# Where the blank rows and the zeros live: a tile moved from the prep's memory to the scatter stage's memory, with its stores

## The chip, the cores and the metric

The kernel runs on one core of one Trainium2 chip. The metric is device time in microseconds (us) of one execution; the median of 10 runs before the change is 7055.33 us (lowest 7051.05, highest 7059.59). Engines are written as the profile writes them: PE (matmul), DVE (vector), ACT (scalar), POOL (GpSimd) and SP (which here only issues transfers). KB in the profile's lists are 1024 bytes; MB and GB/s are decimal.

## The reference, cut to what matters

Four graph layers are computed one after another on 12,500 nodes with 128 features and 200,000 edges; each ends in a layer norm. Only the first layer matters here. It is a weighted sum over edges, grouped by the edge's source node, of rows looked up at the edge's destination node:

```python
def weighted_midpoint_spmm(x_hyp, c, rows, cols, vals):      # rows = src, cols = dst (sorted), vals = edge_weight
    gamma = 2.0 / jnp.clip(1.0 - c * jnp.sum(x_hyp * x_hyp, axis=-1, keepdims=True), EPS)
    gx = gamma * x_hyp
    num = jax.ops.segment_sum(vals[:, None] * gx[cols], rows, num_segments=N_NODES)
    den = jax.ops.segment_sum(vals * (gamma[:, 0] - 1.0)[cols], rows, num_segments=N_NODES)[:, None]
    ...
    return mobius_scalar_mul(0.5, num / den, c)

x = _layernorm(x + _L0_gnn_ref(x, src, dst, edge_weight), axis=-1)
...
```

Layer 2 has a mixture of experts, whose rows are later gathered through a DRAM buffer that must begin as zeros.

## The kernel before

Nodes are held in 98 tiles (`NT`) of 128; edges in 391 blocks (`NB`) of 512. The first layer runs in three stages, one after another.

**Prep** (function `spread_edges`, L489 to L634, and its generator `points`, L452 to L487). The index arrays are loaded, turned to columns by PE transposes (`columns`, L540) and cut into node tile and place within it. A small DRAM round trip (`first_d` stored at L580, read back as `first_r` and `tile_r` at L581 and L583) gives every partition the first node of each block. `rows_d` (L629) puts the rows of indices in DRAM. Then `points` computes the squares of all node rows (`sq`, L469, with sums on DVE at L470), some column arithmetic, and the lookup table `table0`: 14 groups of 7 node tiles, each cut into three bf16 parts (`parts`, L278 to L288: casts on ACT at L283, L285 and L287, differences on DVE at L284 and L286) and stored from SP at L450. The tiles of this loop have two buffers, so that group g+2 starts when the store of group g has landed.

**Scatter** (L636 to L770). For each block of 512 edges: `fetch` (L654) loads the block's indices (`rb`, 256 KB, L656) and 128 rows of the table (`win`, 96.8 KB, L661), both from SP, four buffers each; `places` compares and ranks on DVE; PE picks the rows with one-hot matmuls (L695, L701); ACT casts them into message rows (L734); POOL writes them with four indirect transfers (L751), 128 rows of 792 bytes each, into the DRAM array `msg`. There, each of the 98 source tiles has room for 18 x 128 rows, of which the edges fill only some.

**Collect** (`collect_edges`, L850). All 98 pieces of `msg` are loaded back (`ce_r`, L860) and summed. The first of these loads follows the last scatter.

Rows of `msg` that no edge fills must hold a neutral row. That is the work of the tile `blank` (L516 to L519: four 128-row blocks of zeros, with -1 and 127 in the last columns) and of `clear` (L521 to L524), which stores it with one SP transfer of 396 KB. The last tile's three stores come first (L633 and L634; they cover its blocks 8 to 17), and every other tile's last four blocks are cleared by one call each in `fetch` (L662 to L667). Scatters of the first half of the blocks (`i < MID`) are declared free of a dependence on the clears made in `fetch`, so the scheduler may put these anywhere among them; the first scatter does depend on the last tile's three stores. In the same way the tile `zero` (L639 and L640) is stored 56 times, 448 KB each, into the experts' buffer `buf` (L668 to L670), from SP.

In the scatter loop the order of DVE, PE and ACT is written out by hand (`manual_schedule`, L710). SP and POOL are not in that list: a scheduler orders their transfers, and hoists a store as soon as its source tile is ready in its estimate. A tile's memory matters for that: a tile of the pool `sc` (`pc`) has memory of its own from the start of the prep; a tile of a pool opened after the prep's pools `px` and `rf` are closed takes over memory that these have used, and must wait until it is free.

Of the kernel before, what the change touches and what calls it, by code (L numbers as in the profile page):

```python
# [10 lines left out]
F32 = mybir.dt.float32  # L11
BF16 = mybir.dt.bfloat16
# [6 lines left out]
PSUM = bass.MemoryType.PSUM  # L19
DRAM = bass.MemoryType.DRAM  # L20

P = 128
N = 12500
D = 128
# [11 lines left out]
W0 = D + 2  # L36
# [11 lines left out]
RB = 18  # L48
SURE = 14
SURE_LAST = 8  # L50
RS = RB * P
# [6 lines left out]
W3 = 3 * W0 + 6  # L58
# [80 lines left out]
def gnn_kernel(ctx: ExitStack, tc: tile.TileContext, a, out: bass.AP):  # L139
    nc = tc.nc  # L140
    V, S, G, T, Y = nc.vector, nc.scalar, nc.gpsimd, nc.tensor, nc.sync
# [53 lines left out]
    msg = dram.tile([NMSG, W3], BF16, name="msg")  # L195
# [293 lines left out]
    def spread_edges(bad):  # L489
# [5 lines left out]
        with tc.tile_pool(name="sc", bufs=1) as pc, tc.tile_pool(name="scp", bufs=1, space=PSUM) as pps:  # L495
# [16 lines left out]
            V.memset(rows, 0.0)  # L512
            V.memset(rows[:, :, :, D + 1:D + 2], 1.0)


            blank = pc.tile([P, RB - SURE, W3], BF16, name="blank")  # L516
            V.memset(blank, 0.0)
            V.memset(blank[:, :, 3 * W0:3 * W0 + 1], -1.0)
            V.memset(blank[:, :, 3 * W0 + 1:3 * W0 + 3], 127.0)  # L519

            def clear(t, b0, b1):  # L521
                r0 = t * RS
                return Y.dma_start(msg[r0 + b0 * P:r0 + b1 * P, :].rearrange("(b p) f -> p b f", p=P),
                                   blank[:, 0:b1 - b0, :])  # L524

            if True:
                px_ = ExitStack()
                pt = points(px_.enter_context(tc.tile_pool(name="px", bufs=1)), px_)
# [1 line left out]
                with tc.tile_pool(name="rf", bufs=1) as pa, tc.tile_pool(name="rfp", bufs=2, space=PSUM) as tp_:  # L530
# [25 lines left out]
                    f = pa.tile([P, NBK, EB], F32, name="f_r")  # L556
# [73 lines left out]
                    columns(w_c, w_r)  # L630
                next(pt, None)
                px_.close()
                for b in range(SURE_LAST, RB, RB - SURE):  # L633
                    clear(NT - 1, b, min(b + RB - SURE, RB))  # L634

            with tc.tile_pool(name="sb", bufs=4) as lp, tc.tile_pool(name="sw", bufs=3) as wk, \  # L636
                    tc.tile_pool(name="sg", bufs=2, space=PSUM) as gp:
                step = 7 * D
                zero = pc.tile([P, step], F32, name="zero")  # L639
                V.memset(zero, 0.0)  # L640
                bz = buf[0:DUMP, :].rearrange("(p r) f -> p (r f)", p=P)
                empty = list(range(NT - 1))
                fill = list(range(0, DUMP // P * D, step))
# [10 lines left out]
                def fetch(i):  # L654
                    rb[i] = lp.tile([P, 2 * EB], BF16, name="rb")
                    Y.dma_start(rb[i], rows_d[i].partition_broadcast(P))  # L656
                    _, at = nc.values_load_multi_w_load_instructions(
                        first_r[0:1, i:i + 1], engines=[ET.SP], min_val=0, max_val=NP - 1,
                        skip_runtime_bounds_check_because="clamped to the last node on the chip")
                    win[i] = lp.tile([P, 3, D + 1], BF16, name="win")  # L660
                    Y.dma_start(win[i].rearrange("p k f -> p (k f)"), table0[ds(at[0], P), :])  # L661
                    if 4 <= i < MID - 20 and empty:  # L662

                        for _ in range(-(-NT // (MID - 24))):
                            cl = clear(empty.pop(0), SURE, RB)
                            tc.declare_no_dep(cl.ins, group="spread", reason="rows that no edge has yet")
                            tc.add_to_no_dep_group("blank", cl.ins)  # L667
                    if i % 6 == 5 and fill:  # L668
                        r = fill.pop(0)
                        Y.dma_start(bz[:, r:r + step], zero)  # L670
# [331 lines left out]
    with tc.tile_pool(name="cei", bufs=1) as pi:  # L1002
        ih_i = pi.tile([P, WM], I16, name="ih_i")
        G.iota(ih_i, pattern=[[1, WM]], base=-(WM // 2), channel_multiplier=0)
        V.tensor_copy(iota_h, ih_i)
    spread_edges(bad)
    places_ = ctx.enter_context(ExitStack())
    plp = places_.enter_context(tc.tile_pool(name="places", bufs=1, side="right"))
# [602 lines left out]
```

## Time and profile before

| what | value |
|---|---|
| median of 10 runs | 7055.33 us |
| the profiled execution's own time | 7049.75 us |
| its span, first to last instruction | 7048.0 us |
| prep: first table group's arithmetic (L448) starts | 109.23 us |
| scatter stage: first window load issued, first and last scatter start | 203.65, 212.37 and 2195.1 us |
| collect: first load of `ce_r` | 2197.9 us |
| stores of `blank` (L523): number, first and last issue | 100, 31.9 and 402.5 us |
| stores of `zero` (L670): number, first and last issue | 56, 68.7 and 732.9 us |
| memset of `blank` (L517), of `zero` (L640) on DVE | 718 ns, 805 ns |

How to read it: the span is a little shorter than the time, and it is that of one execution. "Busy" counts an engine's instructions, and the DMA share is the mean busy share of 16 DMA engines; it can exceed 1 in a window. Transfers that SP issues are listed as SPq; an issue that has to wait for room shows as a longer issue, or as a wait of SP for an earlier transfer. A releaser behind `<-` names what ended an idle time.

### The profile page before, as it was taken

Reading aid. Unit: us, or ns where it says so; the run is one execution under the profiler, and the core shown is the slowest. Engines: PE = TensorE matmul, PEld = TensorE weight load, DVE = VectorE, ACT = ScalarE, POOL = GpSimd, SP = SyncE. Lnnn points to the kernel's source line nnn. Section 1 sums busy time; section 2 is a strip of 40 time slices with the busy share of each in tenths; the row PEclk is TensorE's granted clock in tenths of the full one; section 3 lists DMA queues with packets and bytes.
Section 4 is the critical chain, followed back from the end, with each engine's and each line's share of the span. In section 5 each row is a group of like instructions: output and inputs, shape, how many; then the busy total and the mean of one; then the engine's idle time right before and its main releaser. Section 6 shows DMA issues by size and latency. Waiting matters only on the chain. (4 is left out here: it accounts for less than half of the span.)

```text
span 7048.0 us, 106823 instructions
## 1 busy us (share of the span) xinstructions
PE 5168.6 (73%) x33009; PEld 3148.9 (45%) x33009; DVE 4277.1 (61%) x11730; ACT 2016.6 (29%) x4176; POOL 3881.9 (55%) x3917
## 2 busy tenths in 40 slices
PE   0566666666664666699998548998809999699995
PEld 0454444444442333355554336664305544355544
DVE  6787777777775778766665574556991223411115
ACT  3343333333331223333332113444440001100003
POOL 0677777777773000577777570004707776477760
PEclk5555555555556888899999559999959999799998
DMA  9996555555557999355554115554458889698872
GB/s 233 245 244 201 164 152 153 153 152 152 153 153 222 326 324 311 122 166 166 166 165 151 46 56 156 166 165 139 141 156 275 292 287 297 206 291 288 282 229 63
DMA packets 1046138, 1375.96 MB, mean 195 GB/s; under 512 B 106733, under 2 KB 848745, under 8 KB 1045567
## 3 DMA queue, kind: packets, MB, share of 16 engines
q1 hardware_dynamic: 803208, 960.67, 46.3%
q0 software_dynamic: 181312, 376.38, 17.6%
q10 hardware_dynamic: 61046, 31.77, 1.6%
q8 instruction: 301, 4.93, 0.3%
q14 instruction: 271, 2.21, 0.1%
HBM read 911.40 MB, written 457.00 MB: 194 GB/s over the span
## 5 line engine op out<-in xcount | busy, mean ns | idle before, releaser
L1134 POOL DMA_INDIRECT fg<-table,e_row x1952 | 1956.5, 1002 | 1513.7 <-SPq L1023 670.5
L1125 PE MATMUL dense<-fc_a,fc_x 128*128 128x512 bf16 x7644 | 1910.4, 381 | 205.8 <-DMA fc_x<-table 205.5
L751 POOL DMA_INDIRECT msg<-rows,to x1564 | 1505.1, 962 | 672.3 <-issue 360.2
L1125 PEld LDWEIGHTS <-fc_x 128*128 128x128 bf16 x7644 | 678.4, 98 | 797.6 <-issue 195.9
L1227 DVE TENSOR_TENSOR AT<-AT,fps 128x512 f32 x122 | 84.0, 689 | 1489.9 <-PE fps L1151 1489.6
L1089 PE MATMUL fb_ps<-fd,fs 128*128 128x512 bf16 (+4 forms) x4108 | 894.0, 343 | 65.9 <-DVE fd L1075 52.3
L734 ACT CAST rows<-g_ps 128x516 bf16<-128x516 f32 x1173 | 699.6, 596 | 708.4 <-PE g_ps L701 329.1
L701 PE MATMUL g_ps<-rows,minus 128*128 128x258 bf16 x1564 | 463.9, 400 | 584.5 <-ACT rows L734 550.3
L695 PE MATMUL g_ps<-win,hot 128*128 128x129 bf16 x4692 | 650.7, 311 | 265.4 <-DMA win<-table 178.7
L1075 DVE TENSOR_SCALAR fd<-iota_h,hd 128x128 bf16<-128x128 f16 (+6 forms) x1563 | 788.7, 509 | 0.0
L1151 PEld LDWEIGHTS <-fg 128*128 128x128 bf16 x5856 | 464.6, 98 | 520.7 <-DMA fg<-table,e_row 91.0
L695 PEld LDWEIGHTS <-hot 128*128 128x128 bf16 x4692 | 533.2, 143 | 347.0 <-issue 212.6
L1151 PE MATMUL fps<-fh,fg 128*128 128x96 bf16 x5856 | 581.7, 208 | 88.0 <-DMA fg<-table,e_row 65.9
L1476 POOL DMA_INDIRECT yk<-ybuf,come x196 | 218.2, 1113 | 653.5 <-DMA counts<-bc_a 594.1
L868 PE MATMUL ce_sum<-ce_r,ce_s 128*128 128x390 bf16 x1764 | 375.9, 379 | 273.7 <-DVE ce_s L865 269.0
L1089 PEld LDWEIGHTS <-fs 128*128 128x128 bf16 x4108 | 377.8, 98 | 374.9 <-issue 110.8
L1091 ACT CAST fc_a<-fb_ps 128x512 bf16<-128x512 f32 x588 | 344.7, 586 | 633.1 <-PE fb_ps L1089 615.6
L701 PEld LDWEIGHTS <-minus 128*128 128x128 bf16 x1564 | 199.6, 128 | 708.4 <-issue 708.2
L679 DVE TENSOR_TENSOR_SCAN run_ps<-one_ps,run_ps,bin 99x512 f32<-99x512 f32 x390 | 505.5, 1296 | 13.8
L1073 DVE TENSOR_SCALAR fs<-iota_b,hs 128x128 bf16<-128x128 bf16 x1563 | 413.3, 267 | 37.8 <-PE fb_ps L1089 34.2
L868 PEld LDWEIGHTS <-ce_s 128*128 128x128 bf16 x1764 | 188.6, 111 | 461.1 <-DVE ce_s L865 261.2
L1091 ACT CAST bc_a<-fb_ps 128x512 bf16<-128x512 f32 x392 | 227.9, 585 | 451.7 <-PE fb_ps L1089 360.3
(382 smaller groups left out, 6268.8 us busy)
## 6 DMA issues: line engine op xcount, KB each, us to landing
ce_r<-msg SPq DMA_DIRECT2D x98, 1782.0 KB
fc_a<-counts SPq DMA_DIRECT2D x196, 768.0 KB
fc_a<-counts SPq DMA_DIRECT2D x196, 512.0 KB
rb<-rows_d SPq DMA_DIRECT2D x391, 256.0 KB
counts<-fc_a SPq DMA_DIRECT2D x98, 768.0 KB
counts<-bc_a SPq DMA_DIRECT2D x98, 512.0 KB
fc_x<-table SPq DMA_DIRECT2D x490, 96.0 KB
msg<-blank SPq DMA_DIRECT2D x99, 396.0 KB
```

What stands on the lines that cost most here:

```text
L679: V.tensor_tensor_scan(c, one_ps, b, st["end"], OP.mult, OP.add)
L695: T.matmul(gps[i][:, q, 0:D + 1], hot[i][:, q * P:(q + 1) * P], win[i][:, k, :], start=(q == 2 * half and k == 0), stop=False)
L701: T.matmul(gps[i][:, 2 * h:2 * h + 2, 0:D + 1], minus, r[:, 2 * h:2 * h + 2, k * W0:k * W0 + D + 1], start=False, stop=True, skip_group_ch ...
L734: S.copy(r[:, :, k * W0:k * W0 + D + 1], gt)
L751: sc = G.indirect_dma_start(out=msg[:, :], out_offset=bass.IndirectOffsetOnAxis(ap=to[:, q:q + 1], axis=0), in_=r[:, q, :], in_offset=None)
L868: T.matmul(ps, sel[:, j, :], r[:, j, 0:3 * W0], start=(j == 0), stop=(j == RB - 1))
L1075: V.tensor_scalar(col[:, 0:hi - lo], iota_h[:, 0:hi - lo], hd[self.i][:, s, q:q + 1], None, op0=OP.is_equal)
L1089: T.matmul(ps[:, lo - c0:hi - c0], self.sel[s, j], self.col[s, j][:, lo - w[j][0]:hi - w[j][0]], start=(j == first), stop=(j == js[-1]))
L1091: S.copy(out[:, c0:c1], ps)
L1125: T.matmul(dense[n], xr[s][:, k, :], cnt[s][:, n * BANK:(n + 1) * BANK], start=(s == 0 and k == 0), stop=(s == NT - 1 and k == 2))
L1134: G.indirect_dma_start(out=g[q][:, i].rearrange("p k f -> p (k f)"), out_offset=None, in_=table[:, :], in_offset=bass.IndirectOffsetOnAxis ...
L1151: T.matmul(ps[:, ds(at[0], LW)], g[i // 4][:, i % 4, k, :], hot[i // 4][:, i % 4, :], start=False, stop=(i == WC - 1 and k == 2))
```

## The change

`blank` and its memsets, `clear` and the last tile's three clears go from the prep's part of the function to the scatter stage's, into a new pool `late` that is opened after the prep's pools are closed; `zero` moves from `pc` into the same pool. Nothing else is edited: the calls in `fetch` stay.

```diff
-            blank = pc.tile([P, RB - SURE, W3], BF16, name="blank")
-            V.memset(blank, 0.0)
-            V.memset(blank[:, :, 3 * W0:3 * W0 + 1], -1.0)
-            V.memset(blank[:, :, 3 * W0 + 1:3 * W0 + 3], 127.0)
-
-            def clear(t, b0, b1):
...
                 next(pt, None)
                 px_.close()
+
+            with tc.tile_pool(name="late", bufs=1) as lt, tc.tile_pool(name="sb", bufs=4) as lp, tc.tile_pool(name="sw", bufs=3) as wk, \
+                    tc.tile_pool(name="sg", bufs=2, space=PSUM) as gp:
+                step = 7 * D
+                zero = lt.tile([P, step], F32, name="zero")
+                V.memset(zero, 0.0)
+
+                blank = lt.tile([P, RB - SURE, W3], BF16, name="blank")
+                V.memset(blank, 0.0)
+                V.memset(blank[:, :, 3 * W0:3 * W0 + 1], -1.0)
+                V.memset(blank[:, :, 3 * W0 + 1:3 * W0 + 3], 127.0)
+
+                def clear(t, b0, b1):
+                    r0 = t * RS
+                    return Y.dma_start(msg[r0 + b0 * P:r0 + b1 * P, :].rearrange("(b p) f -> p b f", p=P),
+                                       blank[:, 0:b1 - b0, :])
+
                 for b in range(SURE_LAST, RB, RB - SURE):
                     clear(NT - 1, b, min(b + RB - SURE, RB))
-
-            with tc.tile_pool(name="sb", bufs=4) as lp, tc.tile_pool(name="sw", bufs=3) as wk, \
-                    tc.tile_pool(name="sg", bufs=2, space=PSUM) as gp:
-                step = 7 * D
-                zero = pc.tile([P, step], F32, name="zero")
-                V.memset(zero, 0.0)
```

In the built program, the order in which SP issues its transfers changes as follows (counts of transfers issued ahead of a given window load; the first four window loads stand next to each other):

| ahead of window load | blank stores before / after | zero stores before / after |
|---|---|---|
| 1 | 53 / 4 | 9 / 0 |
| 5 | 54 / 5 | 9 / 0 |
| 17 | 68 / 23 | 11 / 4 |
| 41 | 97 / 61 | 16 / 10 |
| 65 | 100 / 99 | 29 / 16 |
| 81 | 100 / 100 | 38 / 36 |
| 117 | 100 / 100 | 56 / 56 |

On DVE, the four memsets move from the prep's first part to a place behind the last group's scaling of the table (L448 and L449) and around the first block's comparison `hot` (L674). POOL's order is the same in both. PE and ACT change places only within the prep, and no engine's order changes behind the scatter stage.

More of the change, by code (lines that the diff above doesn't have):

```diff
@@ L513, in spread_edges @@
             V.memset(rows[:, :, :, D + 1:D + 2], 1.0)
-            blank = pc.tile([P, RB - SURE, W3], BF16, name="blank")
-            V.memset(blank, 0.0)
-            V.memset(blank[:, :, 3 * W0:3 * W0 + 1], -1.0)
-            V.memset(blank[:, :, 3 * W0 + 1:3 * W0 + 3], 127.0)
-            def clear(t, b0, b1):
-                r0 = t * RS
-                return Y.dma_start(msg[r0 + b0 * P:r0 + b1 * P, :].rearrange("(b p) f -> p b f", p=P),
-                                   blank[:, 0:b1 - b0, :])
             if True:
```

## Prediction

> **What bounds the kernel now.** I read the slices first, then the rows of the scatter (L751), then tables by stage, then SP's waits, then the timeline of the handover from prep to scatter. The chain of waits is of no use here: followed back from the end it covers only 44% of the span, and its shares hold no prep and no scatter line.
>
> The last two rows of the slices, each 7048.0 / 40 = 176.2 us long, and the scatter's row among the costliest groups:
>
> ```profile
> DMA  9996555555557999355554115554458889698872
> GB/s 233 245 244 201 164 152 153 153 152 152 153 153 222 326 324 311 122 166 166 166 165 151 46 56 156 166 165 139 141 156 275 292 287 297 206 291 288 282 229 63
> L751 POOL DMA_INDIRECT msg<-rows,to x1564 | 1505.1, 962 | 672.3 <-issue 360.2
> ```
>
> The DMA engines are full in the first three slices and 55% busy from the fifth to the twelfth, where POOL paces the scatter. Four indirect transfers make a block; the stretches below count 632 of them in 800 us, so a block takes 4 x 800/632 = 5.06 us (0.96 us of work and 0.30 us of issue, four times). The collect stage starts 2.8 us after the last scatter (2197.9 against 2195.1), so a microsecond lost before the last scatter is a microsecond of span, unless something hides it.
>
> Now the stretches: columns are the stretch, its length, busy us with counts for PE, PEld, DVE, ACT and POOL, then PE clock, DMA share and GB/s.
>
> ```profile
> 800.00:1600.00 800.00, 497.67 (x3792) 385.91 (x3792) 637.29 (x1583) 316.40 (x633) 607.49 (x632) 0.50 0.57 153
> 100.00:200.00 100.00, 0.00 (x0) 0.00 (x0) 59.74 (x90) 44.45 (x48) 0.00 (x0) 0.50 1.01 229
> 207.85:402.07 194.22, 116.49 (x920) 91.19 (x917) 154.58 (x383) 71.98 (x152) 142.41 (x148) 0.50 1.07 254
> 410.00:430.00 20.00, 12.71 (x102) 10.23 (x103) 16.79 (x43) 7.58 (x16) 15.37 (x16) 0.50 1.00 306
> ```
>
> From 207.85 (window load 5) to 402.07 (window load 42) the DMA engines are full at 254 GB/s, yet POOL issues 148 transfers in 194.2 us, 37 blocks at 5.25 us, and 4.5 us of that is its wait for the first block. The blank stores thus cost nearly nothing in this stage now, but with no room left. SP's own waits from 264 to 402 us say so (in total, times, longest):
>
> ```profile
> SPq L656 <- DMA msg<-blank: 41.2, 17, 4.4
> SPq L661 <- DMA msg<-blank: 16.1, 9, 2.2
> SPq L670 <- DMA msg<-blank: 9.1, 4, 2.8
> ```
>
> SP may issue a transfer when the one eight before it has landed, and the index and window loads stand in the same line as the stores. Half of SP's 138 us there is spent on blank stores that have not landed. The handover, from the timeline (start, duration, engine, line, transfer, count, idle time before it):
>
> ```profile
> 86.64 10.43 SPq L523 DMA_DIRECT2D msg<-blank  x6
> 87.35 1.79 ACT L469 ACTIVATE sq<-xs 128x896 f32<-128x896 f32 x2 [0.31 <-DMA rows_d<-both_r]
> 97.11 1.78 SPq L670 DMA_DIRECT2D buf<-zero  x1
> 98.94 10.42 SPq L523 DMA_DIRECT2D msg<-blank  x6
> 125.07 0.95 ACT L283 CAST parts<-tb 128x903 bf16<-128x903 f32 x1 [7.48 <-DMA table<-parts]
> 195.34 0.39 SPq L450 DMA_DIRECT2D table<-parts  x1
> 203.65 2.91 SPq L661 DMA_DIRECT2D win<-table  x4
> 212.37 1.15 POOL L751 DMA_INDIRECT msg<-rows,to  x1 [193.62 <-DMA msg<-blank]
> ```
>
> The 193.62 us are not a wait for blanks: the first message rows are cast at 212.18. What sets the start is the table, and its groups wait for landings behind blanks.
>
> **Part 1, the prep gets lighter.** 53 - 4 = 49 blank stores and 9 zero stores (0.4055 and 0.4588 MB each) go from ahead of the first window load to behind it. Step by step:
> - `first_d` is issued at 32.38 and waited for until 44.87, with blanks around it, then `tile_r` lands by 50.05, and DVE, which ran dry at 36.85, goes on. Without the blanks I take 5 us less (nothing to 10.5, SP's whole wait). The memsets (0.72 + 0.13 and 0.81 us) leave DVE's prep, and 0.8 us of that lies behind the wait. `both_r` is now made two operations (1.5 us) later. So `rows_d`, issued at 78.66 before, goes out 4.3 us earlier, at 74.4. It landed by 87.3, behind blanks; with an empty queue I take 6 us for its 1 MB, an estimate from `tile_r` (262 KB in 4.9). `sq` waits for it and starts at 80.4 in place of 87.35: **-7 us**.
> - The 14 table groups: first stores issued at 116.6, last at 195.34. Store 1 of a buffer was issued at 116.6, store 7 at 191.81: 12.5 us a round. A round is 5.2 us of ACT and DVE (125.07 to 130.30) and a landing. Landings were 4.8 (167.26 to 172.05) to 9.0 us (156.41 to 165.44); I take 5.2 where nothing is queued, so a round of 10.4: 6 x 2.1 = **-12.6 us**. Bounds: -0 (the landing is no queueing) and -30 (DVE alone, 3.44 us a group, 14 groups in 49 us).
> - At the end, 3 clears of the last tile (1.0 MB) now stand between table stores 12 and 13, and a memset pair (1.65 us) between DVE's last groups; against it, a blank and a zero no longer stand behind store 14. I set **-1.6 us** for the landing of store 14 (8.3 us before).
>
> Window load 5 comes 21 us earlier, at 187 (bounds: 7 to 50).
>
> **Part 2, the scatter stage gets heavier.** From window load 5 to 65, SP now issues 94 blanks and 16 zeros; before, load 5 to 42 had 45 and 7. Each block also loads 0.361 MB (256 + 96.8 KB) and scatters 0.4055. With about 60.5 blocks scattered by then, 60 x 0.361 + 60.5 x 0.4055 + 94 x 0.4055 + 16 x 0.4588 = 91.7 MB, at 254 GB/s **361 us**. A second way, by prices: six blanks and a zero took 12.26 us in the rows above, 1.72 us a blank (some 1.95 a zero); of the 194.2 us, 45 x 1.72 + 7 x 1.95 = 91 go to stores, which leaves 103/37 = 2.79 us a block; after: 94 x 1.72 + 16 x 1.95 + 60.5 x 2.79 = 362 us. POOL alone needs 4.5 + 60.5 x 5.06 = 311 us from window load 5. So 50 us are lost, of which before lost 1 to 2: **+49 us net**. Nothing gives them back: POOL's 5.06 us a block cannot be shortened, and while it starves no backlog builds up. Bounds: 278 GB/s, the best that I found in any 10 us of the full stretch, gives 330 us and +19; 236 GB/s, that of six blanks and a zero alone, gives 388 us and +77. I take 254, from the stretch whose mix is nearest.
>
> After the blanks, 20 zeros stand between window loads 65 and 81, up to 1.5 a block. At 306 GB/s (410 to 430 us, zeros and no blanks) a block with 1.5 zeros takes (0.767 + 0.688)/0.306 = 4.8 us, under 5.06. I take **+2 us**, with bounds 0 and 8. From there on all is as before, later: no other order changes, and DMA is 57% busy.
>
> A rule that speaks against the cost: the Trainium skill, page "DMA: Bandwidth & Descriptors", section "Specifications", gives about 358 GB/s per core as the memory's limit and 512 B as the size from which a transfer runs at line rate; rows of 792 B would qualify. By it, the after's 1.53 MB a block in 5.06 us, 302 GB/s, would fit, nothing would be lost, and the sum would be -20 us (the 21 us and the 1 to 2 that before lost, less 2). The rows above show 254 GB/s at a share of 1.07, so I go by them.
>
> **Sum.** -21 + 49 + 2 = +30 us. The profiled execution took 7049.75 us (span 7048.0), so 7080 for it; the median before is 7055.33, and I put the forecast on that: **7085 us**.
>
> **Rivals.**
> 1. *The stage has room (faster).* One mechanism: the 254 GB/s is what the blocks asked for, not the limit, and SP's waits are latency. Then stores pass beside POOL's 5.06 us a block, and only the earlier start is left. It needs 302 GB/s in full; the sign turns at about 276 (332 us, 21 lost against 21 gained), and 0.2% faster takes some 290. For it: 306 GB/s at 410 to 430 us. Against: that stretch has no blanks, and PE waited for windows in the full one. Full form: -20 us, **7035**.
> 2. *A draw.* The rate is about 265 to 288 with the gain of 21, or 254 with a gain near 50: within 0.2% of before (14 us, about what a measurement here can tell from no change), some **7055**.
> 3. *The prep hardly gains.* The stores are hoisted no more, as the built order shows, but the table rounds are set by landing time itself, not by blanks queued ahead. Gain 7: +44 us, **7099**. For it: a 2 KB load, `first_r`, took 4.1 us too, so 5.2 may be too little. Against: landings of 8 to 9 us exactly where blanks stood ahead.
> 4. *Stores dearer still.* At 236 GB/s, with the zeros at 8: -21 + 76 + 8 = +63, **7118**.
>
> That the change does nothing is ruled out by the order of SP.
>
> **Chances.** Forecast 0.52, rivals 1 to 4: 0.12 each. Slower by over 0.2%: 0.52 + 0.24 = 0.76; within: 0.12; faster: 0.12. The range leaves out rival 1 and the end of rival 4: 7052 to 7114, which is the forecast's own +/-18 and the draw.
>
> **What would show it.** After the change, the DMA share should fall well under 1 between 50 and 170 us; the last table store be issued near 174, the first window load near 182, the first scatter near 191; blanks issue until some 550 us; window loads 5 to 65 be 6.0 us apart, POOL wait for rows in that stretch (some 50 us), and 4 x 800/632 return behind it; the last scatter start near 2225. Wrong would be: blocks at 5.1 us beside 1.57 blanks a block (rival 1), the first scatter later than 200 (rival 3), or a change of more than some us behind the scatter stage, where no order changed.

## The result, and the profile after

The kernel after takes 7097.18 us (median of 8 runs, 7095.61 to 7100.08), the kernel before took 7055.82 us (28 runs) on the same chip: ratio 1.0058, 95% interval 1.0049 to 1.0067. The change makes the kernel slower, 12 us more than forecast and inside the range. The profiled execution took 7093.35 us, its span is 7091.5 us, 43.5 us longer than before.

The page's two last slice rows and the scatter's row, for the kernel after (a slice is 7091.5 / 40 = 177.3 us):

```profile
DMA  4999655555556999455555115554448889698872
GB/s 120 246 244 263 177 152 152 152 152 153 152 152 194 321 324 317 138 165 168 161 169 162 51 56 150 164 163 141 141 150 278 289 286 290 209 291 287 283 232 64
L751 POOL DMA_INDIRECT msg<-rows,to x1564 | 1506.5, 963 | 713.4 <-issue 362.9
```

The first slice, the prep, has fallen from 9 tenths to 4; the second and third are full as before, and the fourth (532 to 709 us), 6 tenths before, is now full too. POOL's work is the same, its idle time 41 us longer. The stretches of the kernel after (stretch, length, busy us with counts for PE, PEld, DVE, ACT and POOL, PE clock, DMA share, GB/s):

```profile
100.00:200.00 100.00, 8.96 (x76) 7.24 (x77) 63.96 (x105) 44.03 (x51) 4.53 (x5) 1.00 0.60 154
190.28:560.06 369.78, 184.36 (x1466) 144.83 (x1465) 250.10 (x613) 116.14 (x245) 233.44 (x243) 1.00 1.07 248
565.00:620.00 55.00, 39.37 (x303) 30.51 (x303) 50.25 (x124) 23.34 (x49) 40.58 (x43) 1.00 1.03 342
800.00:1600.00 800.00, 497.63 (x3774) 385.80 (x3772) 631.65 (x1577) 314.64 (x630) 607.89 (x631) 1.00 0.58 152
```

The second row runs from window load 5 to window load 65: engines full at 248 GB/s, and 243 indirect transfers by POOL. At POOL's pace of 800/632 = 1.266 us each these need 307.6 us. With 4.0 us of wait for the first block, 369.8 - 307.6 - 4.0 = **58 us are lost** here. The last row shows the old pace again, 631 transfers where before had 632. POOL's waits from 194.3 to 560 us, with PE's and DVE's beside them (us in total, times, longest):

```profile
POOL msg L751 <- ACT rows L726: 234.7, 37, 175.8
...
PE g_ps L695 <- DMA win<-table: 130.0, 39, 5.6
DVE hot L674 <- DMA rb<-rows_d: 98.0, 47, 4.6
```

175.8 of POOL's row is the wait for the first block; the other 58.9 us stand in 36 waits (an ordinary pause is 0.3 us, so 48 of them are lost; the other 10 stand in smaller rows, such as 8.9 us in 5 waits for DVE's `g_ps`). The chain behind them is read from the rows below: no message rows, because PE and DVE wait for window and index loads. SP's waits from 264 to 402 us say why these are late:

```profile
SPq L636 <- DMA msg<-blank: 40.4, 22, 3.3
SPq L670 <- DMA msg<-blank: 9.0, 5, 3.4
SPq L656 <- DMA msg<-blank: 8.8, 6, 3.0
```

The handover in the kernel after (start, duration, engine, line, transfer, count, idle time before it; rows between these are left out):

```profile
160.51 0.37 SPq L450 DMA_DIRECT2D table<-parts  x1
162.98 0.81 DVE L627 MEMSET zero<- 128x896 f32 x1 [0.25 <-DVE tb L449]
163.65 0.37 SPq L450 DMA_DIRECT2D table<-parts  x1
163.90 0.72 DVE L630 MEMSET blank<- 128x792 uint32 x1
167.31 0.35 DVE L674 TENSOR_SCALAR hot<-rb,pcol 128x512 bf16<-128x512 bf16 x1 [2.69 <-DMA rb<-rows_d]
168.71 0.95 ACT L285 CAST parts<-rest 128x903 bf16<-128x903 f32 x1 [2.05 <-DVE blank L632]
168.75 1.78 SPq L636 DMA_DIRECT2D msg<-blank  x3
172.36 0.95 ACT L283 CAST parts<-tb 128x903 bf16<-128x903 f32 x1 [2.70 <-DMA table<-parts]
174.18 0.38 SPq L450 DMA_DIRECT2D table<-parts  x1
177.57 0.38 SPq L450 DMA_DIRECT2D table<-parts  x1
178.59 1.15 SPq L636 DMA_DIRECT2D msg<-blank  x1
185.86 2.90 SPq L661 DMA_DIRECT2D win<-table  x4
194.25 1.15 POOL L751 DMA_INDIRECT msg<-rows,to  x1 [175.76 <-ACT rows L726]
```

The last table store goes out at 177.57 (195.34 before), the windows at 185.86 (203.65) and the first scatter at 194.25 (212.37). The last scatter starts at 2237.4 (2195.1): 18 us ahead at the start of the stage, 42 us behind at its end. Behind it 7091.5 - 2237.4 = 4854.1 us remain, against 4852.9 before: no other stage changed its length.

### The profile page after: what moved, and what is told of

It is laid out like the page before. It is cut to its first block, busy times and chain, and to the rows that moved or that the text cites. A ratio compares the mean times of both kernels' runs of the same rounds, so it can differ in the third digit from the quotient of the medians.

```text
span 7091.5 us, 106816 instructions
## 1 busy us (share of the span) xinstructions
PE 5163.1 (73%) x33009; PEld 3142.8 (44%) x33009; DVE 4280.5 (60%) x11730; ACT 2014.4 (28%) x4176; POOL 3883.0 (55%) x3917
## 3 DMA queue, kind: packets, MB, share of 16 engines
q0 software_dynamic: 181312, 376.38, 17.6%
## 5 line engine op out<-in xcount | busy, mean ns | idle before, releaser
L734 ACT CAST rows<-g_ps 128x516 bf16<-128x516 f32 x1173 | 699.7, 596 | 802.7 <-PE g_ps L701 407.6
L695 PE MATMUL g_ps<-win,hot 128*128 128x129 bf16 x4692 | 650.8, 311 | 349.4 <-DMA win<-table 246.9
L695 PEld LDWEIGHTS <-hot 128*128 128x128 bf16 x4692 | 530.7, 143 | 433.0 <-issue 243.5
```

Source lines behind the costliest of these rows:

```text
L695: T.matmul(gps[i][:, q, 0:D + 1], hot[i][:, q * P:(q + 1) * P], win[i][:, k, :], start=(q == 2 * half and k == 0), stop=False)
L734: S.copy(r[:, :, k * W0:k * W0 + D + 1], gt)
```

## Experiments

Theory: while stores of `blank` and `zero` run beside the scatter, the DMA engines are full with rows of 792 bytes, and each store delays the loads by its time in the engines. Rivals: the bytes alone count (A), or a store costs its place in SP's line, whatever the engines do (B). The first four runs shared a chip on which the kernel before took 7043.65 us (22 runs).

**Blank alone moves.** The kernel after, with

```diff
-                zero = lt.tile([P, step], F32, name="zero")
+                zero = pc.tile([P, step], F32, name="zero")
```

> The change with one part undone: zero stays in the prep's memory, only blank moves. In the built order 22 zeros and 4 blanks stand ahead of window load 1; from load 5 to 65 there are 95 blanks and 5 zeros. Throughput theory (the DMA engines are full there, and the loss is the bytes): 95 x 1.72 + 5 x 1.95 + 60.5 x 2.79 = 342 us for those loads, against 311 for POOL alone and 370 measured with the whole change; the start, with zeros behind the table stores, between 194 and 204 us for the first scatter. In all some +15 to +25 us on the kernel before, 7071 to 7081. Rival (the loss is the place of blank stores in SP's line, whatever the bytes): the 95 blanks still stand between the loads, so the loss is that of the whole change, +41 us or more, 7097 to 7105.

Measured: 7074.54 us, ratio 1.0039 (1.0024 to 1.0055). SP now issues 22 zeros in the prep, and 95 blanks and 5 zeros between window loads 5 and 65. Its stretches 186.54 to 527.00 (these two loads) and 264 to 402:

```profile
186.54:527.00 340.46, 180.21 (x1428) 141.69 (x1427) 242.80 (x596) 112.96 (x238) 222.59 (x231) 0.50 1.05 254
...
264.00:402.00 138.00, 66.99 (x537) 52.97 (x537) 92.68 (x226) 42.69 (x91) 86.72 (x90) 0.50 1.08 251
```

Against 7043.65 us on this chip that is +31 us (17 to 39): more than the theory's 15 to 25 and less than the rival's 41. The interval reaches into the theory's range and not up to the rival's. (The expectation's total of 7071 to 7081 was counted from the other chip's 7056, so that 7074.54 falls into it says nothing.) The 340 us for loads 5 to 65 are what the expected prices gave (342). The scatters tell why more was lost: 231 in the stretch, 57.75 blocks and not the 60.5 that I had counted, since the loads run ahead of them. 340.5 - 4.1 - 231 x 800/629 = 42.6 us are lost, not 342 - 311 = 31. The profiled execution was the slowest of its four (7087.61 us) and took 4865.5 us behind the last scatter, where the others of this set took 4853 to 4855; so traces are compared here up to the last scatter only.

**Zero alone moves.** The kernel before, with

```diff
-                zero = pc.tile([P, step], F32, name="zero")
+                zero = lt.tile([P, step], F32, name="zero")
```

and the pool `late` opened for it.

> The other part alone: zero moves, blank stays. 57 blanks and 2 zeros stand ahead of window load 1 (53 and 9 before); load 5 to 42 then has about 40 blanks and 12 zeros. Throughput theory: bytes ahead of the start fall by 4%, and the stretch has 40 x 0.4055 + 12 x 0.4588 MB in place of 45 and 7, nearly the same; within 0.2% of before, 7045 to 7060. Rival (moving the memory itself, with its wait for the prep's tiles, costs): the start comes later by the wait, some us over before.

Measured: 7043.48 us, ratio 1.0001 (0.9992 to 1.0010): no difference, so moving the memory of `zero` costs nothing by itself. The stores of `blank` stay hoisted: 57 of them ahead of the first window load, against 4 in the run above. Against that run, on the same chip, load 5 is issued 12.6 us later (199.13 against 186.54), and the last scatter 31.0 us earlier (2189.3 against 2220.3): -12.6 + 42.6 = +30.0 us is what moving the blanks cost there by these rows, and the medians differ by 31.1 us. Its stretch from 264 to 402 us:

```profile
264.00:402.00 138.00, 85.06 (x650) 65.61 (x651) 108.44 (x271) 53.50 (x109) 103.98 (x109) 1.00 1.04 268
```

Engines full, but POOL at its pace (109 transfers x 1.27 = 138): the same state as before.

**The same bytes in longer runs.** The kernel after, each partition writing four neighbouring rows (3168 bytes) in place of four rows 128 apart (792 bytes each); the same rows of `msg` get the same values:

```diff
-                    return Y.dma_start(msg[r0 + b0 * P:r0 + b1 * P, :].rearrange("(b p) f -> p b f", p=P),
+                    return Y.dma_start(msg[r0 + b0 * P:r0 + b1 * P, :].rearrange("(p b) f -> p b f", p=P),
                                        blank[:, 0:b1 - b0, :])
```

> The changed kernel, with the blank rows stored so that a partition writes its four rows to neighbouring places of msg (one run of 3168 bytes in place of four of 792; all blank rows are alike). Same number of stores, same bytes, same order on SP. Throughput theory in engine time (short runs are dear): the stretch with zeros, 3584 bytes a run, and without blanks ran at 342 GB/s, so a blank falls from 1.72 to about 1.2 us, and a block to 2.79 + 1.57 x 1.2 + 0.27 x 1.4 = 5.05 us: nothing is lost, the earlier start of 18 us stays, 7032 to 7042. Rival A (the limit is bytes written, whatever their runs): as the changed kernel, 7097. Rival B (order in SP's line): as the changed kernel, 7097.

Measured: 7028.82 us, ratio 0.9980 (0.9971 to 0.9989). The order of SP, the number of stores and the bytes are those of the kernel after. Its stretch from 264 to 402 us, and its packets in it:

```profile
264.00:402.00 138.00, 86.74 (x659) 67.11 (x659) 110.35 (x274) 54.40 (x110) 104.78 (x110) 0.50 0.96 304
...
DMA packets 20350, 41.98 MB, mean 304 GB/s; under 512 B 3412, under 2 KB 8616, under 8 KB 20336
```

The packets of the kernel after in the same stretch:

```profile
DMA packets 30404, 34.43 MB, mean 250 GB/s; under 512 B 2813, under 2 KB 25306, under 8 KB 30393
```

More bytes in two thirds of the packets, 304 against 250 GB/s, and POOL is back at its pace: 110 transfers where the kernel after issued 88. Window loads 5 to 65 take 286 us instead of 370; in the kernel before they took 287. Rival A falls, since the bytes did not change, and rival B falls, since the line did not change. From 264 to 402 us SP no longer waits for stores, but for buffers that the engines have yet to free:

```profile
SPq L656 <- DVE bin L677: 43.4, 20, 4.3
SPq L661 <- PE g_ps L695: 24.1, 25, 4.3
```

**The stores spread over the stage's first half.** The kernel after, with about 0.57 blank stores a block and SP's order written out:

```diff
-                    if 4 <= i < MID - 20 and empty:
+                    if 4 <= i < MID - 20 and empty and (i - 3) * 97 // (MID - 24) > (i - 4) * 97 // (MID - 24):
...
-                with tc.manual_schedule(engines={ET.DVE, ET.PE, ET.Activation}):
+                with tc.manual_schedule(engines={ET.DVE, ET.PE, ET.Activation, ET.SP}):
```

> The changed kernel, with SP's order in the scatter loop as written and the 97 clears spread over 171 blocks, 0.57 a block in place of 1.57. Bytes a block: 0.361 + 0.4055 + 0.57 x 0.4055 + 0.17 x 0.4588 = 1.08 MB, at POOL's 5.06 us 213 GB/s, under the 248 measured. Throughput theory: POOL paces the stage from its first scatter, nothing is lost; the first index loads now stand behind the last table store, so the first scatter at some 197 to 202 us in place of 194.3; total 7038 to 7046, faster than before and after. Rival (the blanks' memory or their stores after the prep cost in themselves): still over 7055.

Measured: 7022.53 us, ratio 0.9970 (0.9958 to 0.9982), the fastest. Its row of GB/s by slices, and the stretch from 264 to 402 us:

```profile
GB/s 124 222 215 214 212 210 166 168 167 168 160 153 241 323 319 289 129 166 166 166 166 146 46 56 163 164 167 137 139 156 279 289 289 301 209 292 287 282 228 63
...
264.00:402.00 138.00, 84.80 (x657) 65.95 (x655) 108.69 (x275) 53.33 (x110) 104.93 (x109) 0.50 0.78 212
```

The second to sixth slice now share what the second to fourth had, the engines are at 78%, and POOL is at its pace. The first scatter stays early (186.8 us; zero alone, which equals the kernel before on this chip, starts at 202.4), and the last starts at 2168.2. So what the change gained in the prep is real; it was lost only where the stores were squeezed together. This run changes two things, the spread and who orders SP; the long runs above changed neither of them, and lost nothing either.

**The second set: two other chips.** The next eight runs fell on two chips on which the kernel before takes 8110.99 (23 runs) and 8134.15 us (31 runs). There a block takes about 6.2 us, and the instructions have the same durations. ACT's waits from 800 to 1600 us in the kernel before with long runs, on the second of these chips:

```profile
ACT rows L734 <- remote: 306.8, 71, 6.7
ACT rows L734 <- PE g_ps L707: 74.2, 86, 1.6
ACT rows L734 <- PE g_ps L701: 64.7, 88, 0.7
ACT rows L734 <- DVE to L724: 63.3, 111, 0.8
```

The first row, some 4 us in 71 of the 128 blocks, is a wait for something that the profile can't name; in the kernel before, on the chip of its trace, that row is absent. A block of 6.2 us leaves the engines more time for stores, so these chips say less about the change.

*One store a block*, SP's order written out (the second half of the diff above alone):

> The changed kernel, SP's order in the scatter loop as written: one clear (792-byte runs) a block in place of 1.57, over 97 blocks in place of some 62. Bytes a block 0.361 + 0.811 + 0.076 = 1.25 MB, at POOL's 5.06 us 247 GB/s, just at the 248 to 251 measured where the stretch was full. Throughput theory: on the edge, so window loads 5.0 to 5.2 us apart from load 17 to 101, DMA share near 1, and a time between that of the spread clears and 10 us over it: 0.9968 to 0.9985 of before. Rival (every blank store between loads costs its own latency): 97 clears cost as much as in the whole change, slower than before.

> The kernel after, with SP's order written out as the program has it: one blank store a block from block 4 on, none hoisted among the early blocks, so that about 97 blocks share the 97 stores. The same kernel was tried before on a chip on which a block of the kernel before takes about 6 us in place of 5.06; there the ratio to before was 0.9958, and little could be told. Here, if before lies at 7040 to 7060. Theory (throughput): a block with one store asks for 0.361 + 0.4055 + 0.4055 = 1.17 MB, at 248 GB/s 4.73 us, under POOL's 5.06 us, so the stage loses nothing and the earlier start of 15 to 22 us is kept: ratio 0.9968 to 0.9985, DMA share at 264 to 402 us about 0.95 at some 230 GB/s, last scatter at 2168 to 2185 us. Rival (a blank store costs its place in SP's line, whatever the rate): 97 stores pass the same line, ratio about 1.0058 as in the kernel after.

Measured: ratio 0.9958 (0.9943 to 0.9972) on the first of the two chips, 0.9985 (0.9971 to 0.9999) on the second; the two intervals touch only at 0.9971 to 0.9972. Stretch 264 to 402 us of the second:

```profile
264.00:402.00 138.00, 67.75 (x528) 52.82 (x527) 89.39 (x220) 41.28 (x88) 84.48 (x89) 0.50 0.76 200
```

1.17 MB in 6.2 us is 189 GB/s before any zeros, so the engines are at 76%. Rival B asked for 1.0058, a ratio from the first chip; the kernel after was not run on these two, so this counts for less than the long runs. How much of the gain is kept on a chip with blocks of 5.06 us is open.

*Long runs in the kernel before:*

> The kernel before, with only the blank stores' runs made long (3168 bytes in place of 792, as in the earlier experiment on the changed kernel); tiles stay in the prep's memory. Throughput theory: the 53 blanks ahead of the start cost engine time too, 53 x 0.5 us = some 27 us of transfers in a prep in which the table stores wait behind them; the landings get shorter (6 rounds x 1 to 2 us) and rows_d lands earlier, so the start gains 8 to 15 us: ratio 0.9975 to 0.999. Rival (the prep is set by its own arithmetic and by latency): same as before, 0.9995 to 1.0005.

> The kernel before, with each blank store writing four neighbouring rows from a partition (runs of 3168 bytes) in place of four runs of 792 bytes. Tried before on a chip with blocks of about 6 us, where nothing moved (1.0007). Theory: before lost 1 to 2 us in its scatter stage and some 18 us in its prep to stores; long runs take less time in the DMA engines (304 against 248 GB/s in the changed kernel), so the first scatter comes 5 to 15 us earlier: ratio 0.9975 to 0.999. Rival (stores in the prep cost landing time by their number, not by their time in the engines): first scatter as before, 1.000.

Measured: 1.0007 (0.9991 to 1.0023), then 0.9984 (0.9971 to 0.9998). The second agrees with the theory's figure, the first with the rival's. The first scatter started at 193.0 and 197.9 us, against 212.4 in the kernel before on the chip of its trace, which looks like the theory's earlier start; but no trace of the kernel before exists from these chips, so it is unsettled.

*Spread and long runs together:*

> Spread clears and long runs together, on the changed kernel. Throughput theory: the spread clears are already hidden behind POOL, so the long runs add nothing but the last tile's three stores ahead of the start (1 MB, 1 to 2 us): 0.9965 to 0.997 of before, no faster than the spread alone by over 2 us. Rival (both limits still cost): a gain of another 10 us or more.

> The kernel after with both mends: one blank store for about 0.57 of the blocks over the stage's first half, and runs of 3168 bytes. Each alone gave 0.997 and 0.998 of before on a chip with before at 7044 us; both at once on a chip with blocks of about 6 us gave 0.9998. Theory: with the spread alone the DMA engines were no longer full (share 0.78), so there is nothing left that the long runs could save: ratio 0.9965 to 0.9975, first scatter at 186 to 188 us. Rival (each mend takes away another cost): the gains add up, ratio about 0.995.

Measured: 0.9998 (0.9983 to 1.0013), then 0.9988 (0.9976 to 1.0001), with shares of 0.52 and 0.54. No addition of gains shows, but neither does the gain of either alone. Nothing follows for the first chips.

*Every blank store twice*, the second into a DRAM array that nothing reads:

```diff
+                            k = (NT - 1 - len(empty)) * 4 * P
+                            Y.dma_start(spare[k - 4 * P:k, :].rearrange("(b p) f -> p b f", p=P), blank)
```

> The changed kernel with a second blank store behind each of the 97 clears, of the same size, into a scratch array that nothing reads (extra work that the reference does not need). In the built order, loads 5 to 101 carry 95 clears, 96 scratch stores and 16 zeros. Throughput theory at 249 GB/s: 96 x 0.361 + 96 x 0.4055 + 191 x 0.4055 + 16 x 0.459 = 158.4 MB, 636 us for 96 loads, 6.6 us each, against 486 for POOL: 150 us lost less the 18 of the start, so 128 to 140 us over before. Rival (latency of waiting in SP's line, not bytes): loads 5 to 101 at 6.2 us as after the change, some +85 to +95 us over before.

> The kernel after with a second store of the blank tile, of the same size and shape, behind each clear, into a DRAM array that nothing reads (additional work, the output is that of the reference). Tried before on a chip with blocks of about 6 us: the DMA engines stayed full at 249 to 252 GB/s up to the last blank, but blocks needed most of that time anyway. Theory (throughput): 97 more stores of 0.4055 MB, 39.3 MB at 249 GB/s, are 158 us of engine time; some of it falls in a stretch that has room now, so +128 to +140 us on the kernel after, ratio to before about 1.024 to 1.027. Rival (a store costs only its place in SP's line, about 0.9 us): +85 to +95 us, ratio 1.018 to 1.020.

Measured: 8128.53 us in one run on the first chip, then ratio 1.0055 (1.0035 to 1.0074) on the second, 45 us (28 to 60). Both numbers, the theory's 128 to 140 and the rival's 85 to 95, are missed; both were worked out for blocks of 5.06 us. The stretch from 264 to 402 us, on the first and then on the second chip:

```profile
264.00:402.00 138.00, 67.51 (x520) 52.38 (x520) 86.62 (x214) 41.23 (x88) 80.71 (x84) 1.00 1.04 249
```

```profile
264.00:402.00 138.00, 64.40 (x490) 49.45 (x490) 79.67 (x197) 38.74 (x82) 78.99 (x82) 0.50 1.09 237
```

The engines are full. On the second chip, from window load 5 (190.51) to load 101 (858.13), 96 blocks with 190 blanks and 16 zeros are 96 x 0.767 + 190 x 0.4055 + 16 x 0.4588 = 158.0 MB, at 237 GB/s 667 us; 667.6 were taken. Against 600.9 us for the same loads in the kernel before with long runs, that is 67 us; the last scatter starts 52 us later than there (2689.6 against 2637.1). So here too the length of the stretch fits the bytes over the full rate, and the cost in time is what exceeds the block's own pace.

## Why the prediction was right, point by point

The direction and the mechanism held; three terms were off in size (the table rounds, the landing of store 14, the full stretch). The forecast was 7085 us, 12 us under the median, and the errors add up rather than cancel: it expected too much gain in the prep and too little loss in the stage.

- **The prep up to `sq`: -7.** `first_r` was issued at 39.90 (44.87 before), `rows_d` at 73.85 (74.4 predicted) and `sq` at 79.45 (80.4 predicted): -7.9.
- **Table rounds: -12.6.** ACT began every second group at 113.89, 124.07, 134.59, 144.57 and 155.28, so a round is 10.35 us (10.4 predicted, 12.5 before). The last round failed: store 12 was issued at 163.65 and let the last group start only at 172.36, with two index loads and the three clears behind that store. From the first group's arithmetic (109.23 to 101.33) to the last store (195.34 to 177.57) only 9.9 us more were won.
- **Landing of store 14: -1.6.** It did not come: 177.57 to 185.86 is 8.29 us, 8.31 before. The prediction freed the place behind store 14 of a blank and a zero, but an index load (178.05) and a blank (178.59) came to stand there, with the three clears ahead. Rival 3's landing with a time of its own fails here too: on the other chip this landing took 7.93 us with this order in blank alone (174.19 to 182.12), 6.84 with this order and long runs (171.28 to 178.12), and 5.01 in the spread, with no blank behind it (170.32 to 175.33). The memsets, `hot` (2.69 us for its index load) and ACT's 2.05 us behind them made store 13 late, but store 14 started from the landing of store 12.
- In sum window load 5 came at 190.28, **17.6 us earlier, not 21**.
- **The full stretch: +49.** 361 us were predicted for loads 5 to 65, 369.8 were measured: the 91.7 MB were right, and the rate was 248 in place of 254 GB/s. The rate was taken from a stretch with 45 / 37 = 1.2 blanks a block, and the stretch after had 94 / 60.75 = 1.5. That this is why it is lower is not shown: blank alone, with 95 / 57.75 = 1.6 blanks a block but fewer zeros, ran at 254 on the other chip. Net of the 1 to 2 us that before lost, +56 to +57. Rival 1 (room for 302 GB/s) is refuted for rows of 792 bytes, and rival 4's 236 GB/s was not reached. The bound of 278 GB/s was not quite the best 10 us of the stretch before: 227.85 to 237.85 us ran at 287.
- **Zeros: +2.** Between 565 and 620 us the engines ran at 342 GB/s, and POOL issued 43 transfers where before issued 44: +1.3 at most.
- **SP's line.** That SP issues a transfer when the one eight before it has landed is in the trace: in the kernel before its 2542 transfers signal eight semaphores, 2264 of them the same one as eight transfers earlier, and 96 of the 100 blank stores wait for the one that they will signal.
- **The other signs:** the DMA share fell to 0.10 (50 to 100 us) and 0.38 (100 to 150 us); window loads 5 to 65 stood 6.16 us apart (6.0 predicted), and the last blank store was issued at 560.5 us (some 550 predicted).
- **Sum:** -17.6 + 56.5 + 1 = +40; measured, +42.3 at the last scatter and +43.5 in the span.

The rule of the Trainium skill that spoke against the cost, page "DMA: Bandwidth & Descriptors", section "Specifications" (line rate from 512 B on, about 358 GB/s a core), gave the wrong answer here: with blank rows of 792 bytes the mix filled the engines at 248 GB/s, and the same bytes with blank rows in runs of 3168 bytes went at 304 GB/s with a share of 0.96. The measurement decides.

## What to carry to other kernels

A transfer that looks free has a price that depends on what stands beside it: multiply bytes a block by the rate at which a full stretch of the same mix really runs, and compare with the pace of the engine that sets the stage. Where it exceeds that, don't move the stores as a heap to another place: write longer runs, or spread them until the share falls below 1, and keep the prep free of them as well. Count blocks by the engine that finishes them, not by the loads, which run ahead. How much such a mend gains depends on that engine's pace: 0.2 and 0.3% with blocks of 5.06 us, and between nothing and 0.4%, with no clear order among the mends, on the chips with 6.2 us.

## What the runs showed of the hardware that I had not expected

- In a full stretch packets cost engine time beside the bytes: a third fewer packets with more bytes gave a lower share. From the two packet rows above, with shares of 1.07 and 0.96 of 16 engines, an estimate is 46 ns of one engine's time a packet and 28 us a MB. For blank alone (264 to 402 us, 33266 packets and 34.63 MB) it gives a share of 1.13, where 1.08 was measured; for zeros without blanks (kernel after, 565 to 620 us, 9449 packets and 18.80 MB) 1.09 against 1.03; for the prep's stores in the kernel before (100 to 200 us, 26872 packets and 22.87 MB) 1.17 against 1.01, so it is rough.
- The granted PE clock of the scatter stage stood at 0.50 in some traces (the kernel before, blank alone) and at 1.00 in others (the kernel after, zero alone), while the mean matmul of L695 took 311 ns in the kernels before and after. It has no part in the result: 630 transfers in 800 us come with either.
- The same kernel took 7044 to 7056 us on the first chips and 8111 to 8134 us on two others, with equal durations of the scatter (0.96 us), the cast of L734 (596 ns) and the matmul of L695 (311 ns); whether the chip makes the difference, and what the "remote" wait is stays open.
